# Attention inside a two-FFN block: softmax maxima copied into two PSUM banks by ScalarE instead of added by TensorE, with banks and small transfers rearranged

## The chip, the cores and the metric

One core of one Trainium2 chip. The metric is the device time of one execution in microseconds (us): the median of three runs. A profiled execution of the same kernel stands beside it; its trace is what is read here.

## The reference

Input x is [4, 1024, 128] in float32. Three blocks follow each other:

```python
x = x + 0.5 * ffn(layernorm(x))          # 8 experts, routed by sigmoid weights
x = x + attention(layernorm(x))          # latent Q and K/V, rotary, 16 heads of 64
x = x + 0.5 * ffn(layernorm(x))
```

What matters here is the softmax of the attention: `scores = q k^T / 8`, `attn = softmax(scores)`, `out = attn v`, then the output projection and the residual. The indices of the reference's top-k are not part of the result.

## The kernel before

TensorE, VectorE (DVE), ScalarE (ACT), GpSimd (POOL) and the queue of SyncE (SP, it issues every DMA) run in an order written out by hand: the program issues instructions piece by piece, and each engine takes its own in that order. A kernel-wide method `at(g, fn, place)` puts a piece off to a named place ("mid", "end", "side", "scale", ...) of a later half unit g, and `run_later` (L896) issues what was put there.

The attention is 64 **units** (`for U in range(NUNIT)`, L1157). A unit is 512 queries of a pair of heads. The two heads take the upper and the lower 64 rows of TensorE's array, so that a matmul of one runs beside a matmul of the other. The work of a unit, in the order of TensorE:

- **Scores**, `score` (L926): 8 key tiles of 128 keys, two heads, four matmuls each: three of Q and K halves (high and low parts), and a fourth of a row of ones by a row of negated maxima (`one_row`, `maxr`), which subtracts the maximum. The results stand in six banks in turn, `ps_s0` to `ps_s3`, `psc`, `psx`: tile 0 in `ps_s0` (head 0) and `ps_s1` (head 1), tile 5 in `psc`, `psx`, tile 6 in `ps_s0`, `ps_s1`, tile 7 in `ps_s2`, `ps_s3`. ScalarE takes each by an exponential into `p` (L942), and POOL sums the tiles up in `acc` (L954).
- **Maxima**, `passA` (L901): between the scores, 16 matmuls of a coming unit into the two banks `ps_a`, each reduced by VectorE (L913). `MAXIMA` says between which; `AHEAD` how many slots ahead of the scores they run. The last reduction (L917) gives 128x8 maxima, and `max_row` (L920) takes them by two DMAs through DRAM into a row: `d<-m`, then `maxr<-d`, which scatters single elements.
- **Sides**: after the scores the output matmuls of an earlier unit, `outp` (L985, L997), into `bankO` = `psx`, `ps_s0`, and the rotary up-projection of a coming head, `rope` stage "mm" (L797), into `rope_banks` = `ps_s1`, `ps_s2`.
- **Denominators**, `den` (L967): a matmul of ones by the last unit's `acc` into `ps_s3`, copied by ScalarE to `dsb`, written to DRAM (`d<-dsb`, L980), and gathered transposed into `dT` (L982) in the next unit's "mid". Two half units later VectorE inverts it (L993, waited for by `outp`).
- **Values**, `values` (L956, L962): 16 products of probabilities and latent keys into `psc`, copied to `osb` (L965).
- **Background**: `step` takes pieces of the norms of later batches and of the router of the last FFN, a few a unit: ScalarE norms (L252, L691, L695), TensorE transposes after the values (L707, L759).

Beside the values, ScalarE scales the outputs by the inverse denominators (L1012, eight pieces) and casts the rotation (L820); VectorE does the rotation's products and sums (L810 to L816), adds the outputs to x (L1006) and takes the rotation's low parts (L823). Of the two output adds, head 1's comes ahead of the low parts ("end") and head 0's after them ("late").

Rotations are issued in units 0 to 54, output matmuls in units 2 to 63; the first FFN lies before the attention, the second after it. `bg1` issues the first units' maxima within the first FFN, `bg2` (L1246) the last units' outputs within the second.

Of the kernel before, what the change touches and what calls it, by code (L numbers as in the profile page):

```python
# [24 lines left out]
LOWER = 0.5 - float(np.log(4.0 / 3.0))  # L25
UPPER = 0.5
CENTER = 1.0 / float(np.e)
AHEAD = 15
NSLOT = B * 128
NGRP = NSLOT // 4  # L30
NUNIT = NSLOT // 8
PBUFS = 10
MAXIMA = ((2, 8, 13, 19, 24, 29), (0, 5, 11, 16, 21, 27))
OTHER, VECTOR, PE, NEVER, SCALAR, POOL = 0, 1, 2, 3, 4, 5
NROPE = 9
ACTS = (4, 6, 7)
SWITCH, HOLD = 49, 49
FAR = 8
WLAG, GS, GD = 4, 17, 22
RATE0, RATE1, RATE2, RATE3 = 0.8, 2.8, 2.6, 1.6  # L40
# [7 lines left out]
class Kernel:  # L48
# [10 lines left out]
    def setup(self):  # L59
        nc, tc, ctx, ins = self.nc, self.tc, self.ctx, self.ins  # L60
        pool = lambda name, bufs, **k: ctx.enter_context(tc.tile_pool(name=name, bufs=bufs, **k))
        self.const = const = pool("const", 1)
        self.dram = pool("dram", 1, space=DRAM)
        self.small = pool("small", 2)
        self.prep = pool("prep", 1)

        bank = lambda name: pool(name, 1, space=PSUM).tile([128, 512], F32, name=name)
        self.psA, self.psS, self.psC, self.psX = [bank(f"ps_a{i}") for i in range(2)], [bank(f"ps_s{i}") for i in range(4)], bank("psc"), bank("psx")
        self.rest, self.nrest, self.slot, self.bankO = self.psA, 0, -NSLOT, None
        self.rope_banks = self.psA  # L70

        self.X = const.tile([128, NT, 128], F32, name="X")
        xin = ins["x"].rearrange("(n p) d -> p n d", p=128)
        for n in range(2):
            nc.sync.dma_start(out=self.X[:, 2 * n:2 * n + 2, :], in_=xin[:, 2 * n:2 * n + 2, :])
        self.wrf = const.tile([128, E], F32, name="wrf")
        self.rtemp = const.tile([128, 1], F32, name="rtemp")
        self.tri = const.tile([128, E, E], F32, name="tri")
        self.ident = const.tile([128, 128], F32, name="ident")
        make_identity(nc, self.ident)  # L80
        self.silu = silu = const.tile([128, 1], F32, name="silu")
        nc.vector.memset(silu, 0.0)
        nc.scalar.activation(silu, silu, AF.Silu)
        self.consts = const.tile([128, 4], F32, name="consts")
        for i, c in enumerate((0.5, -CENTER, 1.0, EPS)):
            nc.gpsimd.memset(self.consts[:, i:i + 1], c)
        self.neghalf = const.tile([128, TPB], F32, name="neghalf")
        nc.gpsimd.memset(self.neghalf, -0.5)
        self.ones = const.tile([128, 32], F32, name="ones")
        nc.gpsimd.memset(self.ones, 1.0)  # L90

        self.one_row = const.tile([128, 128], F32R, name="one_row")
        nc.gpsimd.memset(self.f(self.one_row), 0.0)
        for hh in range(2):
            nc.gpsimd.memset(self.f(self.one_row[64 * hh:64 * hh + 1, :]), 1.0)
        self.maxr = [const.tile([128, 512], F32R, name=f"maxr{i}") for i in range(2)]
        for t in self.maxr:
            nc.gpsimd.memset(self.f(t), 0.0)

        self.table = const.tile([128, 3, S], F32, name="table")  # L100
        self.rt = self.prep.tile([128, 4, 512], F32, name="rt")
        self.wr = const.tile([128, 2, 16], F32R, name="wr")
        self.wts = const.tile([128, NT, E], F32, name="wts")
        self.wts2 = const.tile([128, B, E, TPB], F32, name="wts2")
        self.wt_scr = [self.dram.tile([E, S], F32, name=f"wt{b}") for b in range(B)]
        self.q_scr = [[self.dram.tile([4, 4, 32, S], F32R, name=f"qs{b}_{g}") for g in range(4)] for b in range(B)]
        self.k_scr = [[self.dram.tile([4, 4, 32, S], F32R, name=f"ks{b}_{g}") for g in range(4)] for b in range(B)]
        self.c_scr = [[self.dram.tile([128, 2, 512], F32R, name=f"cs{b}_{h}") for h in range(2)] for b in range(B)]
        self.x2_scr = [self.dram.tile([128, 2, S], F32R, name=f"x2_{b}") for b in range(B)]
        self.ckn = [const.tile([128, TPB, 64], F32, name=f"ckn{i}") for i in range(2)]  # L110
# [790 lines left out]
    def passA(self, a, hh):  # L901
# [13 lines left out]
        if m[1] == 16:  # L915
            m8 = self.ms.tile([128, 8], F32R, name="m8")
            nc.vector.tensor_reduce(m8, self.m_of.pop(U)[0].rearrange("p h q k -> p (h q) k"), AX.X, ALU.max, negate=True)  # L917
            self.at(self.group, lambda: self.max_row(U, m8), "mid")

    def max_row(self, U, m):  # L920
        nc = self.nc
        d = self.dram.tile([128, 8], F32, name=f"d3_{U % 4}")
        self.dma(out=d, in_=m)
        self.dma(out=self.maxr[U % 2][0:128:64, :].rearrange("h (q p) -> h q p", p=128), in_=d.rearrange("p (h q) -> h q p", h=2))

    def score(self, s, hh, k):  # L926


        nc = self.nc
        U, c = divmod(s, 8)  # L930
        P, half = divmod(U, 2)
        qs = slice(half * 512, half * 512 + 512)
        ks = slice(c * 128, c * 128 + 128)
        r = slice(64 * hh, 64 * hh + 64)
        Q, K = self.QT[P % 3], self.KT[P % 3]
        ps = (self.psS + [self.psC, self.psX])[(2 * (s % 8) + hh) % 6]
        w, x = ((K[r, 0, ks], Q[r, 0, qs]), (K[r, 0, ks], Q[r, 1, qs]), (K[r, 1, ks], Q[r, 0, qs]), (self.one_row[r, :], self.maxr[U % 2][r, :]))[k]
        nc.tensor.matmul(ps, w, x, start=k == 0, stop=k == 3)  # L938
        if k == 3:
            if hh == 0:  # L940
                self.p_of[s] = self.pp.tile([128, 2, 512], F32, name="p")
            nc.scalar.activation(self.p_of[s][:, hh, :], ps, AF.Exp, scale=0.125)  # L942
            if hh == 1:
                self.accumulate(s)

    def accumulate(self, s):
# [20 lines left out]
    def den(self, U):  # L967

        nc = self.nc
        pd = self.psS[3]  # L970
        parts = [self.p_of[8 * U + c] for c in range(8 - direct(U), 8)] + [self.acc_of[U]]
        for k, part in enumerate(parts):
            for n in range(4):
# [5 lines left out]
        d1 = self.dram.tile([4, 256], F32, name=f"d1_{U % 4}")  # L979
        nc.sync.dma_start(out=d1, in_=dsb[0:128:32, :])  # L980
        g = 2 * U + 4
        self.at(g + (U == NUNIT - 1), lambda: nc.sync.dma_start(out=dT, in_=d1.rearrange("(h x) (y p) -> p (h x y)", x=2, p=128)), "mid")  # L982
        self.at(g + (2 if U == NUNIT - 1 else 1), lambda: self.outp(U, self.osb_of.pop(U), dT), "side")

    def outp(self, U, osb, dT):  # L985
# [8 lines left out]

        def mm(i, hh):
            r = slice(64 * hh, 64 * hh + 64)
            nc.tensor.matmul(po[hh][:, i * 128:(i + 1) * 128], osb[r, i * 128:(i + 1) * 128], self.G[r, j, :], start=True, stop=True)  # L997

        for hh in range(2):
            self.halves[hh] += [lambda i=i, hh=hh: mm(i, hh) for i in range(4)]  # L1000
# [11 lines left out]
                    nc.scalar.activation(po[hh][:, c], po[hh][:, c], AF.Identity, scale=rT[:, 4 * hh + i:4 * hh + i + 1])  # L1012

        self.at(self.group, scale, "scale")
        self.at(self.group, lambda: add(1))
        self.at(self.group, lambda: add(0), "late")

    def run(self):
        nc, tc = self.nc, self.tc
# [39 lines left out]
        with ExitStack() as ctx:  # L1059
# [20 lines left out]
            def bg1(n, point):  # L1080
# [9 lines left out]
                if point == 2 and n >= 64 - AHEAD:  # L1090
# [1 line left out]
                    for hh in range(2):  # L1092
                        self.passA(n - 64 + AHEAD, hh)
                    if n % 4 in (1, 3):
                        self.run_later(self.group, ("mid", "end")[n % 4 // 2])
                if point < 3:
                    return
                if n == FAR:
# [24 lines left out]
        for _ in streams[2].pop() if streams[2] else ():  # L1123
            pass
        assert not (streams[0] or streams[2])
        self.rest, self.rope_banks, self.bankO = [self.psX, self.psS[3]], self.psS[1:3], [self.psX, self.psS[0]]
        flows, needs, blocks = [], {}, list(range(1, B))
        self.attending = True

# [27 lines left out]
        for U in range(NUNIT):  # L1157
# [4 lines left out]

            def rows(hh):
                maxima = lambda i: self.passA(s0 + AHEAD + i, hh) if s0 + AHEAD + i < NSLOT else None
                for n in range(32):
                    if n in MAXIMA[hh]:
                        yield lambda n=n: maxima(MAXIMA[hh].index(n))
                    yield lambda n=n: self.score(s0 + n // 4, hh, n % 4)
                if hh == 1:
                    yield lambda: maxima(6)  # L1170
                for n, fn in enumerate(side[hh]):
                    if hh == 0 and n == 2:
                        yield lambda: maxima(6)
                    yield fn
                if hh == 0 and len(side[hh]) < 3:
                    yield lambda: maxima(6)
                yield lambda: maxima(7)

            for n, pair in enumerate(zip_longest(rows(0), rows(1))):
                for fn in pair:  # L1180
# [2 lines left out]
                if n == 0:  # L1183
                    while self.deferred:
                        self.deferred.pop(0)()
                    for _ in range(2):
                        step(POOL, OTHER)
                if n == 9:
                    self.run_later(2 * U, "mid")
                    rope(U, "high")  # L1190
# [10 lines left out]
                    self.run_later(2 * U, "end")  # L1201
                if n == 26:
                    self.run_later(2 * U + 1, "mid")
                if n == 32:
                    self.run_later(2 * U + 1, "side")
                    rope(U, "side")
            self.halves = [[], []]
# [7 lines left out]
            rope(U, "vector")  # L1215
            self.run_later(2 * U + 1, "end")
            rope(U, "low")
            self.run_later(2 * U + 1, "late")
            rope(U, "end")
            for k in range(8):  # L1220
                self.values(s0 + k)
                if k % 2 == 0 or U < 8:
# [14 lines left out]
        with ExitStack() as ctx:  # L1237
# [6 lines left out]
            g = self.ffn_pre(self.prep, (6, 7), x_of, self.wts2[:, 3].rearrange("p e t -> p t e"), rows=3)  # L1244

            def bg2(n):  # L1246
                for place in ("mid", "side", "scale", "end", "late"):
                    self.run_later(NGRP + 1 + n, place)
                    self.both()
                if n >= GS:  # L1250
# [59 lines left out]
```

## Time and profile before

| | us |
|---|---|
| median of three runs (lowest, highest) | 1622.16 (1620.22, 1623.82) |
| profiled execution | 1621.56 |
| its span, first to last instruction | 1619.70 |
| attention, 240 to 1458 in the profile: PE busy | 1208.6 of 1218 |
| same: DVE, ACT, POOL busy | 1019.1, 877.9, 1098.4 |
| same: mean share of the DMA engines | 0.53 |

In the profile's lines, a group or a piece of time is named by engine, line and tile: "PE psc L962" is a TensorE matmul of line 962 that writes `psc`. PEld is TensorE's load of weights, SPq the queue of DMA issues. The chain of work that ended last is followed back from the end; its pieces are "start us, us, what". In a timeline the columns are start, duration, engine, line, operation, output<-inputs, shapes and count, and in brackets the idle time of the engine ahead of it and what ended it.

### The profile page before, as it was taken

How to read it: one execution, taken by the hardware profiler on the slowest of the kernel's cores; microseconds unless marked ns; L12 is line 12 of the kernel's file. 1: busy time of each engine (PE TensorE's matmuls, PEld its weight loads, DVE VectorE, ACT ScalarE, POOL GpSimd, SP SyncE). 2: the span in 40 equal slices, each digit the busy share in tenths (PEclk: the TensorE clock that was granted, in tenths of full speed). 3: DMA queues.
4: the chain of work that ended last, by engine and by line, in shares of the span. 5: the costliest groups of instructions: out<-in, count | busy, mean ns of one | idle time of the engine just before them, and what ended most of it. 6: DMA issues, size and time to landing. Idle time of an engine off the chain costs nothing.

```text
span 1619.7 us, 31073 instructions
## 1 busy us (share of the span) xinstructions
PE 1570.5 (97%) x10924; PEld 1054.0 (65%) x10924; DVE 1298.5 (80%) x2308; ACT 1115.2 (69%) x2488; POOL 1378.8 (85%) x820
## 2 busy tenths in 40 slices
PE   7998999999999999999999999999999999999998
PEld 5876766666666666566666666666666666556776
DVE  6566678898888889988888898889888866616897
ACT  4675667768777777777777777777677676665554
POOL 5678889989888889988989998989998898994676
PEclk9999999999999999999999999999999999999999
DMA  7025565565555555555555555655665532025543
GB/s 230 1 66 157 156 170 144 133 156 132 144 132 131 153 149 138 150 139 138 132 144 144 133 142 135 166 151 139 152 153 137 130 93 55 2 93 148 140 132 102
DMA packets 241148, 212.27 MB, mean 131 GB/s; under 512 B 157664, under 2 KB 170592, under 8 KB 240224
## 3 DMA queue, kind: packets, MB, share of 16 engines
q1 hardware_dynamic: 240992, 210.28, 50.0%
q8 instruction: 87, 1.43, 0.4%
q14 instruction: 69, 0.57, 0.1%
HBM read 130.39 MB, written 79.82 MB: 130 GB/s over the span
## 4 chain that ended last, share of the span: by engine, by line
PE 82%; DVE 6%; ACT 4%; POOL 3%; DMA 2%; issue 2%; SPq 1%; POOLq 0%; DVEq 0%; ACTq 0%
PE psc L962 25%; PE ps_s L938 21%; PE ps_a L912 8%; PE psc L938 4%; PE ps_s L463 3%; PE psx L938 3%; PE ps_s L543 3%; PE ps_s L797 2%; PE ps_s L997 2%; PE ps_s L974 2%; DVE m L913 2%; PE psx L498 2%; PE psc L434 1%; PE psx L997 1%; PE psc L543 1%
## 5 line engine op out<-in xcount | busy, mean ns | idle before, releaser
L954 POOL TENSOR_TENSOR acc<-acc,p 128x1024 f32<-128x1024 f32 x381 | 907.0, 2381 | 29.8
L913 DVE TENSOR_REDUCE m<-ps_a 128x1 f32<-128x512 f32 x1024 | 671.2, 685 | 161.9 <-PE ps_a L912 138.5
L942 ACT ACTIVATE p<-ps_s 128x512 f32<-128x512 f32 x768 | 411.5, 601 | 66.5 <-PE ps_s L938 42.7
L962 PE MATMUL psc<-p,ckn 128*64 128x512 f32 x2048 | 453.6, 595 | 0.0
L938 PE MATMUL ps_s<-QT,KT 64*128 64x512 f32 x2304 | 420.1, 394 | 0.3 <-DVE C_a L718 0.3
L912 PE MATMUL ps_a<-KT,QT 64*128 64x512 f32 x1024 | 390.1, 413 | 7.6 <-DVE m L913 5.8
L962 PEld LDWEIGHTS psc<-p,ckn 128*64 128x64 f32 x2048 | 141.4, 137 | 282.0 <-issue 282.0
L938 PEld LDWEIGHTS ps_s<-QT,KT 64*128 64x128 f32 x2304 | 284.3, 184 | 57.4 <-DVE X L1006 17.0
L954 POOL TENSOR_TENSOR acc<-p 128x1024 f32<-128x1024 f32 x64 | 153.8, 2403 | 86.8 <-ACT p L942 84.5
L912 PEld LDWEIGHTS ps_a<-KT,QT 64*128 64x128 f32 x1024 | 174.1, 184 | 43.4 <-DVE m L913 17.3
L938 PE MATMUL ps_s<-maxr,one_row 64*128 64x512 f32 x768 | 194.5, 392 | 0.0
L820 ACT CAST hi_r<-ps_s 128x512 fp32r<-128x512 f32 x110 | 64.5, 587 | 122.7 <-DVE ps_s L815 119.5
L938 PE MATMUL psx<-QT,KT 64*128 64x512 f32 x384 | 119.1, 390 | 0.0
L965 ACT COPY osb<-psc 128x512 f32<-128x512 f32 x64 | 37.3, 583 | 111.5 <-PE psc L962 111.5
L938 PE MATMUL psc<-QT,KT 64*128 64x512 f32 x384 | 109.2, 390 | 0.0
L938 PEld LDWEIGHTS ps_s<-maxr,one_row 64*128 64x128 f32 x768 | 102.4, 184 | 10.0
L551 POOL TENSOR_TENSOR p<-eo,p 128x512 fp32r<-128x512 f32 x42 | 62.7, 1499 | 41.5 <-ACT p L550 32.6
L1012 ACT ACTIVATE psx<-psx,rT 128x128 f32<-128x128 f32 x248 | 85.2, 344 | 17.5 <-ACT p L942 11.5
L447 POOL TENSOR_TENSOR X<-X,dtmp 128x512 f32<-128x512 f32 x54 | 69.2, 1281 | 31.7 <-ACT dtmp L446 30.6
L1012 ACT ACTIVATE ps_s<-ps_s,rT 128x128 f32<-128x128 f32 x248 | 84.3, 340 | 6.0
L942 ACT ACTIVATE p<-psc 128x512 f32<-128x512 f32 x128 | 77.4, 605 | 6.7 <-PE ps_a L912 3.3
L942 ACT ACTIVATE p<-psx 128x512 f32<-128x512 f32 x128 | 77.9, 608 | 0.0
(268 smaller groups left out, 2664.0 us busy)
## 6 DMA issues: line engine op xcount, KB each, us to landing
C_l<-cs SPq DMA_DIRECT2D x128, 256.0 KB
QT<-qs SPq DMA_DIRECT2D x256, 128.0 KB
KT<-ks SPq DMA_DIRECT2D x256, 128.0 KB
qs<-hi_r SPq DMA_DIRECT2D x32, 512.0 KB
qs<-eo SPq DMA_DIRECT2D x32, 512.0 KB
ks<-hi_r SPq DMA_DIRECT2D x32, 512.0 KB
ks<-eo SPq DMA_DIRECT2D x32, 512.0 KB
rt<-wt SPq DMA_DIRECT2D x52, 256.0 KB
```

The lines of the kernel that those rows point to most:

```text
L447: nc.gpsimd.tensor_tensor(X[:, t:t + 4, :], X[:, t:t + 4, :], tmp, ALU.add)
L463: nc.tensor.matmul(p, w[:, a, e, :], xs[:, c, :], start=k == 0, stop=k == 2)
L543: nc.tensor.matmul(p, w[:, a, e, :], xs[:, c, :], start=k == 0, stop=k == 2)
L551: (nc.gpsimd if m < N - 1 else nc.vector).tensor_tensor(sh[:, 1, :], hp, self.f(sh[:, 0, :]), ALU.subtract)
L820: nc.scalar.copy(w["hi"][:, k, :], w["ps"][k])
L912: nc.tensor.matmul(self.psA[hh], self.QT[P % 3][r, 0, q0:q0 + 128], self.KT[P % 3][r, 0, kk * 512:kk * 512 + 512], start=True, stop=True)
L913: nc.vector.tensor_reduce(m[0][:, hh, qb, kk:kk + 1], self.psA[hh], AX.X, ALU.max)
L938: nc.tensor.matmul(ps, w, x, start=k == 0, stop=k == 3)
L942: nc.scalar.activation(self.p_of[s][:, hh, :], ps, AF.Exp, scale=0.125)
L954: nc.gpsimd.tensor_tensor(acc, self.p_of[s - 1] if c == 1 else acc, self.p_of[s], ALU.add)
L962: nc.tensor.matmul(self.psC[64 * hh:64 * hh + 64, :], self.ckn[b % 2][:, c, :], self.p_of[s][:, hh, :], start=c == 0, stop=c == 7)
L1012: nc.scalar.activation(po[hh][:, c], po[hh][:, c], AF.Identity, scale=rT[:, 4 * hh + i:4 * hh + i + 1])
```

## The change

1. **Fill.** A new tile `maxb` [128, 2, 512] holds the negated maxima of both heads on every partition. At the end of unit U, ahead of the values, `fill(U + 1)` lets ScalarE copy it into `ps_s0` and `ps_s1`, the banks of tile 0 of the next unit. There tile 0's matmuls are three instead of four, the first with `start=False`, so that they add to what the copy left. This holds for units 1 to 63.
2. **Transfers of the maxima.** `AHEAD` goes from 15 to 16, so a unit's maxima are complete at the end of the unit two before it (it was early in the unit before it). `max_row` spreads the DMAs over the next unit: `d<-m` in a new place "first", the scatter in "mid", then a copy of the row to DRAM in "end" and a broadcast of it to 128 partitions in the second "mid". `MAXIMA` and the place of the eighth maximum are moved forward by up to one place.
3. **Banks.** Outputs go to `ps_s0`, `ps_s1`, rotation to `ps_s2`, `ps_s3`, denominators to `psx`. Both output adds are done together, ahead of the rotation's low parts. The output matmuls clear their bank with the first only.
4. **Gather of the denominators.** `dT<-d` is issued at the end of the unit that made them, in a new place "turn" after the fill.

```diff
-AHEAD = 15
+AHEAD = 16
-MAXIMA = ((2, 8, 13, 19, 24, 29), (0, 5, 11, 16, 21, 27))
+MAXIMA = ((2, 7, 13, 18, 23, 28), (0, 5, 10, 16, 21, 26))
-SWITCH, HOLD = 49, 49
+SWITCH, HOLD = 48, 48
...
     def max_row(self, U, m):
-        nc = self.nc
+        g, row = self.group + 1, self.maxr[U % 2]
         d = self.dram.tile([128, 8], F32, name=f"d3_{U % 4}")
-        self.dma(out=d, in_=m)
-        self.dma(out=self.maxr[U % 2][0:128:64, :].rearrange("h (q p) -> h q p", p=128), in_=d.rearrange("p (h q) -> h q p", h=2))
+        d5 = self.dram.tile([2, 512], F32, name=f"d5_{U % 4}")
+        self.at(g, lambda: self.dma(out=d, in_=m), "first")
+        self.at(g, lambda: self.dma(out=row[0:128:64, :].rearrange("h (q p) -> h q p", p=128), in_=d.rearrange("p (h q) -> h q p", h=2)), "mid")
+        if U:
+            self.at(g, lambda: self.dma(out=d5, in_=row[0:128:64, :]))
+            self.at(g + 1, lambda: self.nc.sync.dma_start(out=self.maxb.rearrange("p h q -> p (h q)"), in_=d5.rearrange("h q -> (h q)").unsqueeze(0).to_broadcast([128, 1024])), "mid")
+
+    def fill(self, U):
+        for s, hh in ((0, 0), (0, 1)):
+            self.nc.scalar.copy(self.bank(s, hh), self.maxb[:, hh, :])
+            self.filled.add((8 * U + s, hh))
...
-        nc.tensor.matmul(ps, w, x, start=k == 0, stop=k == 3)
-        if k == 3:
+        nc.tensor.matmul(ps, w, x, start=k == 0 and not filled, stop=k == last, skip_group_check=filled)
+        if k == last:
...
     def den(self, U):
-        pd = self.psS[3]
+        pd = self.psX
...
-        self.at(g + (U == NUNIT - 1), lambda: nc.sync.dma_start(out=dT, in_=d1.rearrange(...)), "mid")
+        self.at(g - 1 + (U == NUNIT - 1), lambda: nc.sync.dma_start(out=dT, in_=d1.rearrange(...)), "turn")
...
-            nc.tensor.matmul(po[hh][...], osb[r, ...], self.G[r, j, :], start=True, stop=True)
+            nc.tensor.matmul(po[hh][...], osb[r, ...], self.G[r, j, :], start=i == 0, stop=True, skip_group_check=i > 0)
...
-        self.at(self.group, lambda: add(1))
-        self.at(self.group, lambda: add(0), "late")
+        self.at(self.group, lambda: [add(hh) for hh in range(2)])
...
-        self.rest, self.rope_banks, self.bankO = [self.psX, self.psS[3]], self.psS[1:3], [self.psX, self.psS[0]]
+        self.rest, self.rope_banks, self.bankO = [self.psX, self.psS[3]], self.psS[2:4], self.psS[0:2]
...
             rope(U, "low")
-            self.run_later(2 * U + 1, "late")
+            if U + 1 < NUNIT:
+                self.fill(U + 1)
             rope(U, "end")
+            self.run_later(2 * U + 1, "turn")
             for k in range(8):
                 self.values(s0 + k)
```

## The prediction

> **What bounds the kernel now.** I read the page first: the engines' shares and the chain that ended last.
>
> ```profile
> PE 1570.5 (97%) x10924; PEld 1054.0 (65%) x10924; DVE 1298.5 (80%) x2308; ACT 1115.2 (69%) x2488; POOL 1378.8 (85%) x820
> ...
> PE 82%; DVE 6%; ACT 4%; POOL 3%; DMA 2%; issue 2%; SPq 1%; POOLq 0%; DVEq 0%; ACTq 0%
> ```
>
> TensorE is on the chain for 82%. The copies of the 64 units' `osb` (L965) start from 240.5 to 1457.4, so a unit takes 1216.9/63 = 19.3 us, and whatever is saved or added in a unit counts some sixty times. Next I read the chain in order of time in one unit, 789.31 to 808.66:
>
> ```profile
> 789.31 0.43 PE ps_s L938
> 789.74 0.23 PE ps_s L938 x2
> ...
> 797.60 0.70 PE ps_s L938 x7
> ...
> 799.56 0.70 PE ps_s L797 x6
> 800.26 0.23 PE ps_a L912 x2
> 800.49 0.57 PE ps_s L974 x8
> 801.06 7.02 PE psc L962 x32
> 808.08 0.59 PE psx L759 x4
> 808.66 0.43 PE ps_s L938
> ```
>
> Scores with maxima, then outputs and rotation, last maxima, denominators, values, a background piece: TensorE without a hole. So a removed matmul counts in full, and so does every new wait of TensorE.
>
> **Part 1, the removed pair.** Matmuls of the two heads run two at a time: late in the run the chain has 16 score matmuls in 1.85 us (1442.87), 0.231 a pair. 63 units (all but the first) lose one pair: 63 x 0.231 = **-14.6 us**.
>
> **Part 2, the exchanged banks.** Outputs go from `psx`, `ps_s0` to `ps_s0`, `ps_s1`; rotation from `ps_s1`, `ps_s2` to `ps_s2`, `ps_s3`. The last key tile's scores stand in `ps_s2` (head 0) and `ps_s3` (head 1). So the rotation's second half now waits for the very last exponential of the unit, before for the one ahead of it. What such a wait costs is seen in unit 1, which has no output matmuls, so that rotation comes close behind the scores (ScalarE's and the weight loads' timelines):
>
> ```profile
> 250.13 0.60 ACT L942 ACTIVATE p<-ps_s 128x512 f32<-128x512 f32 x1
> ...
> 250.78 0.18 PEld L797 LDWEIGHTS ps_s<-C_l,wup 64*128 64x128 f32 x1 [0.37 <-ACT p L942]
> ```
>
> The exponential ends at 250.73 and the weight load follows 0.05 later; TensorE's order is kept, so everything behind waits too. In the usual unit:
>
> ```profile
> 798.88 0.59 ACT L942 ACTIVATE p<-ps_s 128x512 f32<-128x512 f32 x1
> ...
> 799.28 0.53 PEld L797 LDWEIGHTS ps_s<-C_l,wup 64*128 64x128 f32 x6
> ```
>
> The last exponential ends at 799.47, so the load that now goes at 799.28 can go at 799.52: 0.24 late. Scores, exponentials and what stands between them and the rotation all move forward together when the pair goes, so this gap stays. TensorE can run head 0's stream meanwhile, but it then has one matmul of head 1 alone at the end, a slot of 0.23; the two estimates agree. 53 units with rotation and outputs: 53 x 0.24 = 12.7; units 0 and 1 wait one whole exponential longer (250.13 to 250.62 = 0.49): 1.0. Together **+13.7** (bounds 12 and 16, by 0.05 us in the release). Head 1's outputs wait likewise for an exponential that ends at 798.32 (797.72 + 0.59); their load went at 798.14, but head 0 is the slower stream there. In the nine units without rotation I take 0.03 each, **+0.3** (0 to 1.5). So the pair's gain is handed back at the end of the same scores.
>
> **Part 3, two copies on ScalarE.** A full-bank copy takes 0.59 (L965), two in a row 1.1. Their place: the rotation's casts end at 806.10 (804.91 + 1.19); VectorE's two output adds now follow at once, 0.60 apart behind the row at 804.79, the second ending at 806.66; so copy 1 runs from 806.15 and copy 2 from 806.7 to 807.3. Values run until 808.08. Cover of 0.8 us: in a plain unit the copies cost nothing. If it were gone, each 0.1 us late would cost 6 us. ScalarE's queue behind them holds background norms, then `osb`. Where TensorE's transposes wait for norms, the copies count. Of the twelve units with transposes (24 each of L707 and L759, four a unit) the timeline shows four whose chain is ScalarE's already:
>
> ```profile
> 395.92 0.59 ACT hi_r L820
> 396.51 0.20 ACT mv L691
> 396.71 0.02 issue
> 396.74 1.65 ACT X L695 x4
> 398.39 0.17 ACT ya L252
> 398.56 0.12 issue
> 398.68 1.26 ACT ya L252 x3
> 399.94 0.04 issue
> 399.98 0.33 PE psx L707
> ```
>
> Here the copies go between the cast and the next piece: 4 x 1.1 = 4.4. In five others four norms end at 807.64, just ahead of the transposes at 808.01; they would end at some 808.7, and as transposes follow norm by norm only the last is late, 0.2 to 0.5: 5 x 0.35 = 1.7. Three have cover. **+6.1** (2 to 8).
>
> **Part 4, the maxima's transfers.** On SP's queue the copy out, the scatter, a new 4 KB copy and a new broadcast of 512 KB follow each other, each waiting for the one before. The trace has no such broadcast. Rows of the two first steps:
>
> ```profile
> 849.84 0.34 SPq L57 DMA_DIRECT2D d<-m  x1
> 851.30 0.57 SPq L57 DMA_DIRECT2D maxr<-d  x1
> 851.97 3.37 SPq L57 DMA_DIRECT2D qs<-hi_r  x1
> ```
>
> A small step takes 1.5 us on an idle queue, 4.0 behind loads (1025.22 to 1029.24), and the DMA behind the scatter is out only 4.0 after it. A 256 KB broadcast is used 3.5 us after its issue (1460.33 to 1463.84), and 512 KB may take twice that. Chain: 1.5 to 4, + 4, + two stores 2 to 3, + 1.5 to 4, + 3.5 to 7: 12.5 to 22 us. It may start at the end of the cycle before, 1 to 2 us ahead of the scores, and has until 17.5 after their start, 18.5 to 19.5 in all: likely in time, cost **0** (0 to 27, see the rivals). DMA engines at a share of 0.53 take the 33 MB more (63 times 512 KB). The Trainium skill, "DMA: Bandwidth & Descriptors", section Anatomy of one DMA (for the other issue path), gives 2 us fixed and 436 GB/s: by it the four would take 9.2 us, never late; here the queue ahead decides. Its "PSUM — Partial Sum Buffer", The four PSUM rules, speaks against the change: any seed but 0 should go through TensorE by a matmul. Done so, the pair of Part 1 would return and the sum be 14.6 us higher. No row here shows a matmul upon ScalarE's writing.
>
> **Part 5, the rest.** Denominators in `psx`: that bank's last exponential is long done; 0. The gather a third of a cycle earlier: SP stands until `d` has landed (842.33 to 844.20), behind it only the next cycle's first copies; it removes one late gather (unit at 982: outputs to rotation 991.43 to 993.21 against 798.13 to 799.31, 0.6) and one in the tail (VectorE waits 0.82 at 1474.34): **-1.4**. One more pair of maxima before the attention, one fewer in unit 62: TensorE even; two VectorE reductions of 0.69 more in a stage where TensorE is busy 52.6 of 57 us: **+0.3** (0 to 1.4). Maxima packed closer: VectorE waits for TensorE's maxima 119.7 us in the attention, 1.9 a unit, so it follows; 0 (0 to 6).
>
> **Sum:** -14.6 + 13.7 + 0.3 + 6.1 - 1.4 + 0.3 = **+4.4** on the profiled execution's 1621.56 (span 1619.70 and 1.86 around it): 1626.0. It stands 0.6 under the median, 1622.16, so 1626.5.
>
> **Rivals.** *The waits don't bite (faster).* For it: TensorE holds two streams, and only one is stopped; the pair is gone for certain. Against it: unit 1's row. If rotation slips in at no cost and the norms cost 1.7: -14.6 - 1.4 + 1.7 = -14.3, 1608; with a third of the wait 1612. It decides where less than 0.1 us of Part 2's 0.24 is left.
> *The broadcast is late (slower).* For it: in every second unit four key loads stand in the queue ahead of the scatter, and stores behind it. Against it: today's copy out waits for maxima made 2 us into the unit, the new one doesn't. ScalarE would wait with everything behind, and TensorE for the first tile's bank. Half a us to a us in some 27 units: +14 to +27 on the sum: 1640 to 1653. It decides where landing is later than 17.5 us into the unit.
>
> **Chances.** Forecast 0.57, its own range 1619 to 1633; the waits don't bite 0.25 (1606 to 1616); broadcast late 0.18 (1634 to 1653). 0.2% is 3.2 us, about what can be told from no change. Of the forecast 0.32 lies above 1625.4, 0.22 within, 0.03 below 1618.9. Slower 0.32 + 0.18 = 0.50, same 0.22, faster 0.25 + 0.03 = 0.28. The range 1609 to 1641 leaves out the far part of both rivals.
>
> **What would show it.** Part 1: one pair fewer a unit on L938's ones row. Part 2: rotation's weight loads with idle time released by the exponentials, in some 55 units, 0.2 to 0.3 each; wrong if they go at the old distance from the last score. Part 3: copies of 0.59 ended before the values end; norms before transposes later by a us. Part 4: no idle time of ScalarE released by a DMA to the broadcast's tile; if there is, the second rival. The prediction is wrong if a unit without background is clearly shorter than now (18.78 us from 490.61 to 509.39, between two starts of the values).

## The result, and the profile after

The changed kernel takes **1673.53 us** (median; 1671.57 to 1677.96), the kernel before beside it 1622.97: **+50.6 us**, a ratio of 1.0318 (95% interval 1.0293 to 1.0344). Forecast were 1626.5 and a range up to 1641. The side was right and the size wrong by 47 us.

The page after, its engines and chain, and two of its groups (columns: line, engine, operation, shapes, count; busy us, mean ns of one; idle time of the engine ahead of them and what ended it):

```profile
PE 1593.2 (95%) x10798; PEld 1029.6 (61%) x10798; DVE 1305.1 (78%) x2308; ACT 1187.4 (71%) x2614; POOL 1378.7 (82%) x820
...
PE 69%; DVE 9%; DMA 9%; ACT 5%; POOL 4%; issue 2%; SPq 1%; POOLq 0%; DVEq 0%; ACTq 0%
...
L954 PE MATMUL ps_s<-maxr,one_row 64*128 64x512 f32 x642 | 171.9, 401 | 0.0
...
L937 ACT COPY ps_s<-maxb 128x512 f32<-128x512 f32 x126 | 72.7, 589 | 53.5 <-DMA maxb<-d 43.9
```

TensorE does 126 matmuls fewer, as promised (the row of ones by the maxima into `ps_s`: 768 before, 642 now), and yet it has fallen from 82% of the chain to 69%; DMA has risen from 2% to 9%. Ahead of its 126 copies ScalarE stood 43.9 us for the broadcast. The list of waits of the same kernel (engine, tile and line; released by; us in total, times, longest) has a second one that is new in size:

```profile
PEld ps_a L914 <- DVE m L915: 59.8, 189, 2.4
ACT ps_s L937 <- DMA maxb<-d: 43.9, 23, 9.3
```

The first was 17.3 us before: TensorE's maxima now wait for VectorE's reductions.

I measured each unit in both traces: from the first to the last score matmul ("scores"), from there to the first value ("sides"), and from the last value's start to the next unit's first score ("gap"). Units 0 to 62 together: scores +14.0 us, sides +13.2, gaps +24.4; unit 0 starts 4.1 later (0.7 to 3.0 of it also in five kernels with the same program up to there, runs 3, 10 and 12 to 14 below). That is 55.7 together and not 50.6, since the profiled execution was the changed kernel's longest, 1677.96. A plain unit, the one from 516.34 before and from 539.03 after: scores 8.69 to 8.54, sides 3.10 to 3.31, together 18.80 to 18.87. So the sides grow by as much as the prediction said, the pair brings 0.15 instead of 0.23, and most of the loss (44.4 of 51.5 us) is in 24 units that are each longer by more than 0.6.

One such unit in the chain after, in order of time; it answers the piece of before at 395.92 to 399.98:

```profile
461.98 4.88 DMA maxr<-d
...
466.88 3.57 DMA d<-maxr
...
470.51 4.33 DMA maxb<-d
...
474.92 1.11 ACT ps_s L937 x2
476.02 0.24 ACT mv L693
...
476.29 1.65 ACT X L697 x4
477.93 0.78 ACT ya L254 x2
...
478.76 1.25 PE psx L709 x3
480.00 0.72 PE ps_s L954
```

The unit's scores start at 455.5; the scatter goes only 6.5 later, behind four key loads, and the three transfers take 12.8 us. They land at 474.84, 19.3 after the start, 2.4 later than the copies begin in a plain unit (16.95). Then everything stands in ScalarE's line: copies, norms, and TensorE's transposes at 478.4, after 3.92 us without a matmul. What such a hole costs beyond itself is seen in the stretches behind it (window: length, busy us and instructions of PE, PEld, DVE, ACT, POOL; then PEclk, DMA share, GB/s):

```profile
480.00:482.00 2.00, 2.00 (x11) 1.62 (x12) 1.07 (x2) 0.78 (x1) 0.00 (x0) 0.50 0.19 1
...
484.00:486.00 2.00, 2.00 (x14) 1.61 (x12) 0.96 (x3) 1.03 (x3) 1.09 (x1) 0.65 0.84 265
486.00:488.00 2.00, 2.00 (x20) 1.68 (x18) 1.73 (x3) 1.98 (x4) 1.92 (x2) 1.00 0.97 240
```

TensorE's granted clock is 0.50 until 485, and a pair of score matmuls takes 0.43 us instead of 0.23: that unit's scores are 2.33 longer.

### The profile page after: what moved, and what is told of

It is laid out like the page before. It is cut to its first block, busy times and chain, and to the rows that moved or that the text cites. A ratio compares the mean times of both kernels' runs of the same rounds, so it can differ in the third digit from the quotient of the medians.

```text
span 1676.2 us, 31099 instructions
## 1 busy us (share of the span) xinstructions
PE 1593.2 (95%) x10798; PEld 1029.6 (61%) x10798; DVE 1305.1 (78%) x2308; ACT 1187.4 (71%) x2614; POOL 1378.7 (82%) x820
## 4 chain that ended last, share of the span: by engine, by line
PE 69%; DVE 9%; DMA 9%; ACT 5%; POOL 4%; issue 2%; SPq 1%; POOLq 0%; DVEq 0%; ACTq 0%
PE ps_s L954 18%; PE psc L979 16%; PE ps_a L914 7%; PE psc L954 4%; DMA maxb<-d 4%; PE ps_s L465 4%; PE ps_s L545 3%; PE psx L954 3%; PE ps_s L1014 3%; DVE m L915 2%; DMA maxr<-d 2%; PE ps_s L799 2%; PE psx L500 2%; DMA d<-maxr 2%; PE psx L991 1%
## 5 line engine op out<-in xcount | busy, mean ns | idle before, releaser
L914 PE MATMUL ps_a<-KT,QT 64*128 64x512 f32 x1024 | 407.0, 427 | 18.9 <-DVE m L915 15.5
L954 PE MATMUL ps_s<-QT,KT 64*128 64x512 f32 x2304 | 412.5, 399 | 12.3 <-ACT ps_s L937 11.0
L954 PEld LDWEIGHTS ps_s<-QT,KT 64*128 64x128 f32 x2304 | 276.5, 188 | 80.1 <-ACT ps_s L937 31.5
L1029 ACT ACTIVATE ps_s<-ps_s,rT 128x128 f32<-128x128 f32 x496 | 164.4, 341 | 22.2 <-ACT p L959 9.7
L954 PE MATMUL ps_s<-maxr,one_row 64*128 64x512 f32 x642 | 171.9, 401 | 0.0
L937 ACT COPY ps_s<-maxb 128x512 f32<-128x512 f32 x126 | 72.7, 589 | 53.5 <-DMA maxb<-d 43.9
L1023 DVE TENSOR_TENSOR X<-ps_s,X 128x512 f32<-128x512 f32 x124 | 85.2, 687 | 30.9 <-ACT ps_s L1029 24.6
L954 PEld LDWEIGHTS ps_s<-maxr,one_row 64*128 64x128 f32 x642 | 87.9, 186 | 8.7
L1014 PEld LDWEIGHTS ps_s<-G,osb 64*128 64x128 f32 x992 | 87.6, 186 | 4.2 <-ACT p L959 1.3
L1014 PE MATMUL ps_s<-G,osb 64*128 64x128 f32 x992 | 88.6, 279 | 0.4 <-ACT p L959 0.3
```

The costliest lines, as they stand in the source:

```text
L914: nc.tensor.matmul(self.psA[hh], self.QT[P % 3][r, 0, q0:q0 + 128], self.KT[P % 3][r, 0, kk * 512:kk * 512 + 512], start=True, stop=True)
L937: self.nc.scalar.copy(self.bank(s, hh), self.maxb[:, hh, :])
L954: nc.tensor.matmul(ps, w, x, start=k == 0 and not filled, stop=k == last, skip_group_check=filled)
L1023: nc.vector.tensor_tensor(x, po[hh].rearrange("p (t d) -> p t d", t=4), x, ALU.add)
```

## The experiments

Differences are against the kernel before on the same chip (1622.16, 1624.29, 1624.17 and 1623.35 us in the four sets); each is uncertain by some 2 to 4 us (95% intervals). "Unit sums" are over units 0 to 62 in the profile, so of one execution each.

**1 and 2. The broadcast's wait, then its transfers, taken away.**

```diff
+        self.maxc = const.tile([128, 2, 512], F32, name="maxc")   # memset to -1000
-            self.nc.scalar.copy(self.bank(s, hh), self.maxb[:, hh, :])
+            self.nc.scalar.copy(self.bank(s, hh), self.maxc[:, hh, :])
```

> The changed kernel, but the two copies read a tile that holds the constant -1000 from the start; the copy to DRAM and the broadcast still run, into a tile that nobody reads. So the maxima of the first key tile are left out, and ScalarE waits for no broadcast. Theory (the broadcast lands late): ScalarE's 43.9 us of idle time before the copies, in 23 waits, go; the gaps ahead of a unit's scores that are longer than a norm's copies explain (some 14 us) and most of the scores that are over 8.7 us long behind them (some 18 us) go too: 1673.5 - 32 = 1641, 1634 to 1652. Rival (ScalarE's and VectorE's queues are the cause, the wait for the DMA only stands in front of another): within 8 us of the changed kernel, 1665 to 1674.

> As the one before, and the copy of the row to DRAM and the broadcast are left out (the maxima of the first key tile too). Theory (what costs is only the wait for the landing): within 5 us of the kernel with the constant, 1641. Rival (33 MB more in the queues, and SyncE standing until the row's copy has landed, also delay other transfers): 8 to 20 us below the kernel with the constant.

Measured: 1658.40 (+36.2) and 1659.25 (+37.1). The wait for the landing is worth **14.3 us** (50.6 - 36.2), not 32, and the 33 MB of traffic nothing that can be told. The theory holds for less than half. Where a part of the rest comes from is seen in one unit of the first of them (VectorE's and TensorE's timelines):

```profile
1134.13 0.95 DVE L347 RECIPROCAL dx<-dx 128x128 f32<-128x128 f32 x1 [1.37 <-ACT dx L339]
...
1135.68 0.49 PE L916 MATMUL ps_a<-KT,QT 64*128 64x512 f32 x1 [1.06 <-DVE m L917]
```

The scores began at 1132.74. A background reciprocal of VectorE waits for ScalarE, whose router pieces stand behind the copies; the first reductions of maxima wait behind the reciprocal; TensorE stands 1.06 us for them. I had followed the copies to the transposes only.

**3. The banks alone**, on the kernel before:

```diff
-        pd = self.psS[3]
+        pd = self.psX
-... self.psS[1:3], [self.psX, self.psS[0]]
+... self.psS[2:4], self.psS[0:2]
```

> The kernel before with the exchange of banks alone: outputs in ps_s0 and ps_s1, rotation in ps_s2 and ps_s3, denominators in psx, both output adds together. Theory (the rotation's second half waits for the unit's last exponential): 0.24 us in 53 units and 1 us in the first two, +13.7: 1636.5, 1634 to 1638. Rival (the wait is there only because the missing pair let the scores end earlier, or the other head's stream covers it): 1620 to 1626.

Measured: 1633.49, **+11.3** (ratio 1.0075, 1.0060 to 1.0090); sides +12.3 in the unit sums. The forecast was +13.7, and the time lies just under its range; the cost is there without any pair removed.

**4. Rotation where it waits for no last exponential**, in the changed kernel: `rope_banks` is `psX`, `psS[2]`, denominators in `psS[3]`.

> The changed kernel with the rotation in psx and ps_s2 and the denominators back in ps_s3, so that the rotation waits for no exponential but the last one of head 0. Theory: the time from the last score to the first value goes back from 3.31 to 3.07 us in 53 units, -12.7: 1661, 1658 to 1665. Rival (ScalarE is behind anyway, so that the next step of its queue, the scaled outputs and the rotation's casts, is late instead): 1670 to 1676.

Measured: 1676.97, no gain. The unit sums of the sides go from +13.2 to +8.8, and TensorE's weight loads in a plain unit show what stands there now:

```profile
547.12 0.19 PEld L914 LDWEIGHTS ps_a<-KT,QT 64*128 64x128 f32 x2 [0.35 <-DVE m L915]
```

The last maxima wait for VectorE: one wait has taken the other's place. The 8.8 that stay are what the eighth maximum's place costs the sides by itself (8.9 in run 10, 9.0 in run 14). Neither theory nor rival had this. The 4.4 us that the sides gain are not in the time; scores and gaps are 2.8 longer than in the changed kernel.

**5. Two transfers fewer.** The first writes the maxima to DRAM in the order of the row; row and broadcast both read from there.

```diff
-        self.at(g, lambda: self.dma(out=d, in_=m), "first")
+        self.at(g, lambda: self.dma(out=d5.rearrange("h (q p) -> p h q", p=128), in_=m.rearrange("p (h q) -> p h q", h=2)), "first")
```

> The changed kernel with two steps fewer between the maxima and the broadcast: the first transfer writes the maxima into DRAM in the order of the row, then the row and the broadcast are both read from there, one behind the other. Theory (the chain of transfers is what makes the broadcast late): ScalarE's idle time before the copies goes, and the time comes to that of the kernel with the constant, 1658, 1654 to 1662. Rival (a scattered write to DRAM takes longer than the scattered read did, and everything behind it in the queue is late): 1672 or more.

Measured: **1883.24**. The rival, by far. The DMA queue's own waits:

```profile
SPq L57 <- DMA d<-m: 572.6, 64, 11.9
```

SyncE stands 8.9 us each time until 1024 single elements are written to DRAM (the 128 rows of 32 bytes took it 2.2 in the changed kernel: 128.5 us in 58 waits).

**6. No copies.** The changed kernel without `fill`: four matmuls in every tile again.

> The changed kernel without the two copies, all four matmuls back in the first key tile; banks, transfers and the broadcast (into a tile that nobody reads) as changed. Theory (the copies push ScalarE's background work, through it VectorE's, through it the maxima of the next scores, and the late broadcast acts through them): the gaps (24.4 us) and most of what the scores have gained (14 us) go, the banks' 13 us stay: 1636, 1630 to 1643. Rival (transfers or closer maxima cost as much): 1655 or more.

Measured: 1653.24, **+29.0**. Gaps -0.1 in the unit sums, as the theory says, but scores +14.4: something that isn't ScalarE's costs there. Between theory and rival, close to the rival.

**7. The old places of the six maxima** among the scores, in the changed kernel.

> The changed kernel with the old places of the maxima among the score matmuls. Theory (VectorE doesn't follow the closer maxima, which takes some 0.1 us of the removed pair's 0.23 in a plain unit): 55 units by 0.1, -5.5: 1668, 1664 to 1671; a plain unit's scores 8.45 us for 8.55. Rival (the places change nothing): 1671 to 1677, plain scores at 8.55.

Measured: 1677.95, no gain, though the plain unit's scores take 8.46: there the pair is worth its full 0.23. The sides grow to 3.38 in return, and the gaps by 1.9 in the unit sums.

**8. The copies behind the background pieces:**

```diff
             for k in range(8):
+                if k == 7 and U + 1 < NUNIT:
+                    self.fill(U + 1)
                 self.values(s0 + k)
```

> The changed kernel with the two copies behind the unit's background pieces in ScalarE's order, ahead of the last product of values. Theory (it is what stands behind the copies that costs): background norms and the reciprocals that wait for them come at their old times, and the broadcast has longer in those units: some 22 us below the changed kernel, 1651, 1645 to 1660. Rival (the copies are then late for the first scores in the same units by as much): 1668 or more.

Measured: 1665.04, -8.5 on the changed kernel, between theory and rival. Scores fall from +14.0 to +1.2 in the unit sums (among others the reciprocals are in time again); the gaps stay at +24.7. Now the copies are late where a piece ahead of them waits (run 9, without broadcasts, shows gaps of +13.6 from that alone), and in five other units, 11.9 us together, the broadcast is still late.

**9. What the idea could bring at best:** 8 with a constant tile, no transfers, and the places and banks of 7 and 4.

> What the idea could bring at best: the changed kernel with the copies from a constant tile behind the unit's background pieces, no copy of the row and no broadcast (the maxima of the first key tile are left out), the old places of the maxima, and the rotation in psx and ps_s2 with the denominators in ps_s3. Theory (costs add up as the runs so far show them): 63 pairs -14.6, sides +8.8, nothing for maxima, transfers or queues: 1617, 1611 to 1624. Rival (two copies a unit cost as much behind the background pieces as ahead of them): 1632 or more.

Measured: 1647.66, **+23.5**: the rival. ScalarE's timeline shows why copies can't simply be put behind the pieces:

```profile
365.66 0.30 ACT L233 ACTIVATE rstd<-mv,consts 128x4 f32<-128x4 f32 x1 [3.05 <-DVE mv L229]
...
365.96 1.09 ACT L935 COPY ps_s<-maxb 128x512 f32<-128x512 f32 x2
```

A norm's piece waits 3.05 us for VectorE's statistics, and the copies with it; the next scores start 2.1 us late. In the unit sums the gaps are 13.6 longer where the theory had nothing. That is not all: the sides are 15.5 longer for 8.8, and the scores only 6.5 shorter for 14.6.

**10, 13, 14. Closer maxima alone**, on the kernel before: both moves, the six alone (`MAXIMA`), the eighth alone (after the sixth side matmul).

> The kernel before with the closer places of the maxima alone (the six among the scores one place earlier where the change has them so, the eighth after the sixth side matmul). Theory (VectorE doesn't follow): the scores grow by 14 us in all as in the changed kernel without its copies: 1636, 1630 to 1641. Rival (it is the slot more of lead, not the places): 1621 to 1627.

> The kernel before with the six maxima among the scores one place earlier, the eighth in its old place. Theory (two costs of the closer maxima: these take 0.1 us of each unit's scores): +6.3, 1630, 1627 to 1632. Rival (all 14 us come from here): 1636 or more.

> The kernel before with the eighth maximum after the sixth side matmul, the six in their old places. Theory (VectorE, still at the seventh, holds TensorE ahead of the denominators: 0.17 us in 53 units): +9, 1632, 1629 to 1634. Rival (its place changes nothing): 1621 to 1627.

Measured: 1638.34 (**+14.2**), 1630.76 (+7.4), 1630.06 (+6.7): the two add up. Waits of the kernel with both, then of the kernel before:

```profile
PEld ps_a L912 <- DVE m L913: 75.8, 246, 1.0
```

```profile
PEld ps_a L912 <- DVE m L913: 17.3, 37, 1.1
```

No single wait is long; there are four of some 0.3 us in each unit. The six cost 0.1 us of the scores, the eighth 0.17 of the sides. In the unit sums of run 10 that is scores +6.8 and sides +8.9: the theory had the total right, but not that all of it would be in the scores. So the places explain under half of the 14.4 us by which the scores grew in run 6.

**11. The lead alone:** `AHEAD` 16 on the kernel before, transfers a unit later.

> The kernel before with the maxima one slot further ahead alone (16 for 15), their two transfers in the same place of the unit behind. Theory (the places cost, not the lead): 1621 to 1627. Rival (the lead costs: VectorE's first reductions stand behind the unit's last rotation and adds): 1630 or more.

Measured: 1741.22, and neither reading answers it. Plain scores are as before, but a dozen other units' are some 0.2 us longer and unit 0's 2.2, +4.8 in the unit sums: the lead does cost something. In unit 0 its first maxima need keys of the next pair of heads that have not landed; in the changed kernel too TensorE stands 2.10 us there, until `KT<-ks` lands. The sides grow by 101.7 us, VectorE waiting 98.0 us in 33 waits for `dT<-d`. In this order the gather stands on SP's queue behind the maxima's copy and scatter in "mid". In the changed kernel the gather goes earlier, and two such waits are left. So the earlier gather, which I took for a small gain, is what makes the lead possible.

**12. Two copies alone**, on the kernel before, from SBUF to SBUF, at the place of the copies.

> The kernel before with two copies of 128x512 more on ScalarE in each unit, from one SBUF tile to another, ahead of the background pieces; nothing waits for their result and they wait for nothing. Theory (the copies' 1.1 us go through ScalarE's background pieces to the transposes and through VectorE's reciprocals to the maxima): 20 us, 1642, 1636 to 1648. Rival (only the transposes that the prediction counted): +6, 1625 to 1631.

Measured: 1633.68, **+9.5**, between the two. Gaps +6.3 in the unit sums, in just the nine units that the prediction counted (1.0 to 1.2 in the four, 0.4 in the five); scores +4.8: 2.1 in the two units where a reciprocal of VectorE waits for ScalarE's router pieces, 1.5 in three where VectorE's norm statistics (L223 in the kernel before) wait for ScalarE's norms, and 1.3 in one at a granted clock of 0.50.

**15, 16. Can the pair be kept?** Copies and broadcast in 43 units only, behind the pieces, six maxima in old places, rotation as in 4; in 16 the eighth maximum back too.

```diff
-                if k == 7 and U + 1 < NUNIT:
+                if k == 7 and U + 1 < NUNIT and U not in SKIP:
```

> The changed kernel with copies and broadcast in 43 units alone, those in which neither ScalarE's pieces nor the transfers made them late so far; copies behind the pieces, six maxima in their old places, rotation in psx and ps_s2. Theory (43 pairs of 0.23 gained, sides 0.28 us longer in 53 units for the eighth maximum's place): 1622 - 10 + 15 = 1627, 1623 to 1633. Rival (copies and broadcasts are late in other units instead): 1638 or more.

> The kernel of the chosen units with the eighth maximum back in its old place too. Theory (the eighth maximum is what makes the sides longer): 1622 - 10 and up to 4 us of sides: 1614, 1611 to 1619, below the kernel before. Rival (head 1's outputs now wait in ps_s1 for tile 6's exponential, so the sides stay 0.2 us longer in 53 units; or the later maxima make the broadcasts late): 1623 or more.

Measured: 1635.54 (+12.2) and 1631.79 (+8.4; ratio 1.0052, 1.0039 to 1.0065). Both theories fall, the second to its rival. In 16 a plain unit with copies has scores 0.23 shorter and sides 0.15 longer, without copies its sides are 0.05 shorter than before: the shorter scores are followed by longer sides even where no bank waits for the last exponential. Whether it is the rival's wait, for tile 6's exponential, the profile doesn't show. Some 0.1 us a unit stays, and units with pieces, with a late broadcast or with the lead's longer scores eat it. No version beat the kernel before.

## Why the prediction was right or wrong

| step | forecast, us | measured, us | from |
|---|---|---|---|
| 1 removed pair | -14.6 | -14.5 | 63 x 0.23, plain unit of 7 |
| 2 banks | +14.0 | +11.3 | 3, alone |
| 5 closer maxima | 0 (0 to 6) | +14.2 | 10, alone |
| 3 copies in ScalarE's queue | +6.1 (2 to 8) | +21.8 | 36.2 of 1, less (29.0 of 6 - 14.5) |
| 4 late broadcast | 0 (0 to 27) | +14.3 | changed kernel less 1 |
| gather, lead, start | -1.1 | +3.5 | what is left of 50.6 |

The rows don't simply add up. Banks and closer maxima hold TensorE at the same place: alone they make the sides 12.3 and 8.9 longer in the unit sums, together 13.7 (run 6). So some 7.5 us are counted twice, and the last row is small only because it takes them off again: in it stand the lead's 4.8 in the scores (run 11) and some 4 us of run 6's scores whose cause stays open.

**Right:** the pair's size, the exchange that hands it back (so the rival that its waits don't bite is out), and the sign. The row that answers the prediction's 798.88 and 799.28, in a plain unit after:

```profile
546.89 2.25 ACT L959 ACTIVATE p<-ps_s 128x512 f32<-128x512 f32 x4
```

```profile
549.19 0.29 PEld L799 LDWEIGHTS ps_s<-C_l,wup 64*128 64x128 f32 x3
```

The last exponential ends at 549.14 and the rotation's next weights load 0.05 later; the sides are 0.20 to 0.28 longer in nearly all units with rotation and outputs, for a forecast 0.24. The profile marks no idle time there, because the other head's loads run meanwhile: I should have named the length of the sides as the sign, not the weight loads' idle time.

**Wrong, first: "Maxima packed closer: VectorE waits for TensorE's maxima 119.7 us in the attention, 1.9 a unit, so it follows; 0."** An idle sum over a unit says nothing on whether two reductions of 0.68 us fit between two neighbouring maxima. Each is late by 0.1 to 0.3 us, and TensorE, in order, stands. Alone this costs as much as the pair brings (14.2 for 14.5); in the changed kernel it takes 0.08 of the pair's 0.23 in a plain unit's scores, and its part in the sides is mostly covered by the banks' wait. It comes with the pair: `MAXIMA` counts steps in a list that is one shorter, so none of the six goes ahead of the score matmul that it stood before, but the missing pair brings two of them closer. Run 7 moves the six back and pays in the sides.

**Wrong, second: Part 3's list of who stands behind the copies.** The transposes were priced well (6.3 measured alone). Missed were VectorE's reciprocals and norm statistics that wait for ScalarE's pieces (2.1 and 1.5 alone), the second copy's wait for the second output add (0.2 in each unit; the nine gaps are 3.2 longer in 1 than in 12, some 1.9 of it by this wait), and the halved clock behind holes (in the attention 6.8 us lost in 1, 1.7 each in 12 and in 6, none before). Some 6 of the 21.8 are not told apart.

**Wrong, third: Part 4's choice of 0.** The rival had the mechanism, the sign and, at its lower edge, the price (14 to 27) right. The steps were near their terms (4.88, 3.57, 4.33 us); what I mis-set was the start. In most odd units the scatter waits behind four key loads until 3 to 8 us into the unit, and I had let the chain begin 1 to 2 us ahead of the scores. One unit alone is worth 5 us: in the last but one the row's copy stands behind the reload of the FFN's weights, issued at 1481.79 and landed only at 1491.4, and ScalarE waits 9.30 us. The prediction's 9.2 us for four such transfers, an estimate from the Trainium skill's "DMA: Bandwidth & Descriptors", Anatomy of one DMA, lie under the 12.8 that three took here.

The range failed since it let one rival be true at a time and had the closer maxima at 0: VectorE, ScalarE and the transfers were late at once.

## What to carry to other kernels

Before work is moved to an idle engine, follow its in-order queue past the first waiter: ScalarE's pieces fed VectorE's, VectorE's fed TensorE's. Idle time summed over a cycle is no cover; look at the spacing of neighbouring instructions. If what follows a shortened stretch waits for another engine, as the sides here wait for the exponentials and the last maxima, expect most of the gain back there: in run 16, 0.20 of 0.23 us.

## What the runs showed of the hardware

**The clock after a hole.** TensorE's granted clock fell to 0.50 for 3.4 or 6.8 us at holes of 1.4 to 5.4 us. In the attention it cost 10.2 us in the changed kernel (1 less the granted clock, summed over the busy time of stretches of 1 us), nothing before. It isn't a matter of the hole's length alone: in run 1 four holes of 1.72 to 1.74 us ahead of the same transposes brought it three times, and 2.56 us in the changed kernel at 715.7 did not. The five falls in the changed kernel's attention, at 413.7, 478.6, 782.4, 888.2 and 1492.3, lie whole multiples of 3.413 us apart. The Trainium skill, "TensorE: Matmul & The Clock Gate", Part 1, has half rate after an idle window of about 3.4 us that runs freely. That the moment decides agrees; that 1.7 us without a matmul can be enough (1.37 in run 12) differs, unless the four transposes behind (1.6 us) count as idle too, which no run here separates.

**Single elements to DRAM.** Writing 1024 elements one by one made SyncE wait 8.9 us (run 5), while the scatter of as many into SBUF took 4.88 in the chain above. The Trainium skill, "DMA: Bandwidth & Descriptors", Specifications, says that transfers under 512 bytes are read, modified and written. No run here tests it: the rows of 32 bytes, which took 2.2, lie under it too.
